# A four-layer decoder: layer 2's experts in a hand-written order with two result tables, routing steps at the units' ends, shared experts spread, the activation table load tied

## Chip, cores and metric

One core of one Trainium2 chip runs the program. The metric is the device time of one execution in microseconds (us); smaller is better. TensorE is called PE, VectorE DVE, ScalarE ACT, GpSimd POOL and SyncE SP, as in the profile.

## What is computed

The reference is a pre-norm decoder of four layers on x, 128 sequences of 64 positions and 128 features, so 8192 tokens. Every layer adds a self attention, a cross attention to `ctx_1024` and a feed-forward part to x, each of them applied to the layer norm of x. The feed-forward parts differ:

- Layer 0: 64 experts with 64 hidden features; each token goes to 8 of them, chosen within the best 4 of 8 groups of experts; and a shared expert for all tokens.
- Layer 1: a quantised gated layer with 512 hidden features.
- Layer 2: 16 experts with 512 hidden features, where each expert chooses 1024 tokens, and a shared expert with 256 hidden features.
- Layer 3: an inner block with attention, and 8 experts of which the best two count for each token.

Layer 2's experts are the centre of this case:

```python
scores = jax.nn.sigmoid(h @ gate_w.T)
cap = math.ceil(T / E * TOP_K)            # 8192 / 16 * 2 = 1024
topk_score, topk_ids = jax.lax.top_k(scores.T, cap)
xin = h[topk_ids]
up = jnp.einsum('ecd,efd->ecf', xin, up_w) + up_b[:, None, :]
g = jnp.einsum('ecd,efd->ecf', xin, gw) + gb[:, None, :]
eo = jax.nn.silu(g) * up
eo = jnp.einsum('ecf,edf->ecd', eo, down_w) + down_b[:, None, :]
flat = (eo * topk_score[..., None]).reshape(-1, Dm)
out = jnp.zeros_like(h).at[topk_ids.reshape(-1)].add(flat)
```

## The kernel before

x stays in SBUF as 64 row tiles of 128 tokens (`self.x`). Four tiles make a group (G = 4, 512 tokens), so there are 16 groups (`ng`).

**The chains.** `chain` runs the attention parts of a layer one behind the other, as a software pipeline over groups; its unit `u` is half a group. It runs under a manual schedule: every engine issues its instructions in the order in which the code emits them. For each unit it emits the weights (scores and exponentials), the maxima of the next unit, the mix with the values, the division, and, a few groups ahead, the norms (`measured` and `normed`), the transposes (`turned_in`) and the projections (`projected`). Layer norm's statistics come from DVE (lines 190 and 191), the reciprocal root from POOL (193 and 195), and the normalisation itself either from DVE (`norm`, line 215) or from ACT (`norm_act`, line 203 ff.). A chain can carry hooks: functions with a place (half, offset in units), at "a" or "b" within a unit, that do the feed-forward part's routing for a group while the attention of later groups goes on. `chain` takes a function `before`, called ahead of its loop. `feed` and `fed` load the result tables of a previous expert part and add them to x. ACT's table of functions is preloaded once per chain, by `preload_act_table_set`.

**Layer 0's experts.** `l0_ahead` makes the routing hooks. `l0_experts` runs inside the `before` of layer 1's chain, so in the same manual order. The loop takes two experts at a time: `fetch` gathers rows by an indirect DMA (line 1136), `turn` transposes them, `hidden` and `result` are the matmuls, and the results are added into two tables in DRAM by indirect DMAs with addition (line 1143), one table for either slot. The layer's shared expert is a generator whose steps are placed between these. Before the loop, layer 1's attention weights, biases and relative-position tables are prepared.

**Layer 2's experts.** After layer 2's chain, the framework's scheduler sets the order. `l2_places` finds each expert's threshold by 30 bisection steps, the ranks, and the rows that each place of an expert holds. `l2_shared` computes the shared expert and writes x to a table `rows_x` in DRAM. `l2_experts` then goes over 16 experts and two halves of four blocks of 128 tokens each. For a half it emits this:

```python
for k in range(HB):
    self.gather(xe[k], rows_n, idx[:, e, b + k : b + k + 1])
    nc.tensor.transpose(px[:, k, :], xe[k][:, 0:P], self.ident)
```

Then come the 16 hidden matmul instructions (lines 1826 and 1830), a Silu on ACT (1834), the product on DVE (1835), the result matmuls of 128 columns (1845), and four scatters with addition into the one table `rows_x`:

```python
y = sp.tile([P, P], F32, tag=f"y{k}", name=f"y{k}")
nc.vector.tensor_scalar_mul(y, py[:, k, :], xe[k][:, P + e : P + e + 1])
self.scatter_add(rows_x, y, idx[:, e, b + k : b + k + 1])
```

Gathers and scatters are issued by POOL's queue, in its order. At the end x is read back from `rows_x`, and layer 3's chain starts.

Of the kernel before, what the change touches and what calls it, by code (L numbers as in the profile page):

```python
# [8 lines left out]
F32 = mybir.dt.float32  # L9
# [52 lines left out]
class Decoder:  # L62
# [135 lines left out]
    def norm_act(self, dst, src, stats):  # L198
# [4 lines left out]
        nc.vector.scalar_tensor_tensor(  # L203
            out=nb, in0=mv[:, :, 0], scalar=-1.0, in1=rs, op0=ALU.mult, op1=ALU.mult
        )
# [31 lines left out]
    def chain(self, name, subs, hooks=None, before=None):  # L237
# [20 lines left out]
        with ExitStack() as c:  # L258
            pool = lambda *a, **k: c.enter_context(tc.tile_pool(*a, **k))
            c.enter_context(tc.manual_schedule())  # L260
            wp = pool(name=f"{name}_w", bufs=1)
            with tc.tile_pool(name=f"{name}_pw", bufs=2, space=PSUM) as self.pS:
                subs = [sub(wp) for sub in subs]
            if before is not None:
                before()
# [5 lines left out]
            nc.scalar.preload_act_table_set("natural_log_exp_and_others")  # L271
# [8 lines left out]
            for q in groups[-self.ng :]:  # L280
                q["hooks"] = {**q.get("hooks", {}), **(hooks or {})}
# [4 lines left out]
            def feed(q):  # L286
                if q["n"] < self.ng:
                    q["fed"] = []
                    for i, table in enumerate(tables):
                        add = self.gp.tile([P, G, P], F32, tag=f"fed{i}", name=f"fed{i}")  # L290
                        self.load_rows(add, table, q["g"], nc.scalar)
                        q["fed"].append(add)

            def fed(q):
                if q["n"] < self.ng:
                    xg = self.x[:, q["g"] * G : (q["g"] + 1) * G, :]
                    for add in q.pop("fed"):
                        nc.gpsimd.tensor_tensor(out=xg, in0=xg, in1=add, op=ALU.add)

            def hooked(half, u):  # L300
                for q in groups[max(0, (u - far) // 2) : u // 2]:
# [4 lines left out]
            for u in range(-10, max(nu + 6, nu + far - 1)):  # L306
# [4 lines left out]
                if odd:  # L311
                    if not linear:
                        do(self.normed, e + 3)
                else:
# [4 lines left out]
                    if not linear:  # L319
                        do(self.measured, e + 3)  # L320
# [10 lines left out]
                if odd:  # L331
                    do(self.finished, e - 1)
                    if linear:
                        do(self.normed, e + 3)
                    do(self.projected, e + 2)
                    do(self.biased, e + 2)
                else:
                    do(self.valued, e + 1)
                    do(self.turned_in, e + 2)
                    if linear:  # L340
                        do(self.measured, e + 3)
# [3 lines left out]
                if unit(u + 1):  # L345
                    self.turn_maxima(u + 1, unit(u + 1))

# [58 lines left out]
    def projected(self, q):  # L406
# [20 lines left out]
        for r in range(4):  # L427
            for h in range(4):
                rows = slice(r * 32 + h, (r + 1) * 32, 4)

                queue = nc.scalar if q["n"] == 0 and r % 2 else nc.sync
# [284 lines left out]
    def l0_attn(self, wp):  # L716
# [20 lines left out]
        for k in ("rel", "rel_r"):  # L737
            rel = wp.tile([H, 8, P], F32, tag="small", name=f"{k}_sb")
            rel = rel.rearrange("h a (b d) -> h (a b) d", d=HD)[:, 0:127, :]
            nc.sync.dma_start(out=rel, in_=self.t[k])  # L740
# [1245 lines left out]
```

## Time and profile before

| | us |
|---|---|
| median of 3 runs | 4540.99 |
| lowest and highest | 4539.59, 4547.18 |
| the profiled execution | 4533.17 |
| its span | 4531.4 |
| busy: PE, DVE, ACT, POOL | 3695.3, 2748.6, 1999.5, 1716.0 |
| busy: scatters (1143), gathers (1136) | 203.6, 201.8 |

The profile page covers one execution. Its groups give, after the bar, the busy time in us, the mean of one instruction in ns, and the idle time of the engine ahead of it with what ended it ("<-"). A timeline row is start, duration, engine, line, operation, output and inputs, count, and in brackets the idle time before. In the 40 slices a digit is the busy share in tenths; PEclk is the clock that PE was granted, in tenths of full speed. Everything that the prediction rests on comes from that one execution, whose own time stands in the table beside the median.

### The profile page before, as it was taken

The page shows a single profiled execution, that of the slowest core. Times are in us where ns is not written, and L with a number is a line of the kernel's source. Part 1 is how long each engine was busy: PE and PEld are TensorE (multiplying, and loading weights), DVE is VectorE, ACT ScalarE, POOL GpSimd, SP SyncE. Part 2 cuts the span into 40 slices and gives each one's busy share as a digit, 9 for nine tenths or more (in the row PEclk, how much of TensorE's full clock was granted, in tenths as well). Part 3 has the DMA queues.
Part 4 walks back from the last instruction along what each step waited for, and adds up shares of the span by engine and source line. Part 5 has one row for each costly group of instructions (what it writes and reads, how often), then busy time and mean ns, then how long its engine had stood idle before and what let it go on. Part 6 is the DMA issues. An engine that isn't in the chain of part 4 may idle for free. (4 is left out here: it accounts for less than half of the span.)

```text
span 4531.4 us, 157084 instructions
## 1 busy us (share of the span) xinstructions
PE 3695.3 (82%) x67053; PEld 2334.7 (52%) x67053; DVE 2748.6 (61%) x8132; ACT 1999.5 (44%) x3021; POOL 1716.0 (38%) x2762
## 2 busy tenths in 40 slices
PE   5999884776999885447999887688875899889979
PEld 3665552333555553224666654355443566556656
DVE  4665664445777996886556647333321666678766
ACT  2555552112444443334777773111111686447822
POOL 2333554675332444001222222355554223863221
PEclk9999996557999997568999999888887899999989
DMA  3112223342111221000011112122232211101111
GB/s 86 36 42 65 81 77 80 83 80 65 51 41 44 64 61 44 1 1 29 31 36 59 63 57 75 50 52 52 52 58 33 70 35 43 45 30 51 50 50 36
DMA packets 262678, 233.12 MB, mean 51 GB/s; under 512 B 66974, under 2 KB 191031, under 8 KB 261981
## 3 DMA queue, kind: packets, MB, share of 16 engines
q1 hardware_dynamic: 167996, 157.44, 11.1%
q0 software_dynamic: 35104, 29.41, 4.5%
q10 hardware_dynamic: 58880, 36.22, 2.7%
q8 instruction: 530, 8.68, 0.8%
q14 instruction: 168, 1.37, 0.1%
HBM read 93.13 MB, written 58.47 MB: 33 GB/s over the span
## 5 line engine op out<-in xcount | busy, mean ns | idle before, releaser
L610 ACT ACTIVATE p<-st 128x1024 f32<-128x1024 f32 x512 | 522.2, 1020 | 479.6 <-PE st L588 453.7
L575 PE MATMUL st<-qx,kT 64*64 64x256 f32 x9216 | 652.1, 392 | 68.3 <-ACT p L605 37.2
L515 DVE TENSOR_REDUCE m<-ps 128x8 f32<-128x512 f32 x896 | 555.0, 681 | 251.4 <-PE ps L500 250.7
L575 PEld LDWEIGHTS st<-qx,kT 64*64 64x64 f32 x9216 | 324.3, 133 | 231.5 <-issue 60.4
L522 POOL CAST mx<-m 128x32 bf16<-128x32 f32 x256 | 54.5, 213 | 1002.9 <-DVE m L515 1002.8
L628 PEld LDWEIGHTS po<-p,vx 128*32 128x32 f32 x18432 | 287.4, 110 | 224.8 <-issue 221.9
L628 PE MATMUL po<-p,vx 128*32 128x64 f32 x18432 | 380.9, 223 | 0.8 <-ACT p L610 0.8
L193 POOL TENSOR_SCALAR ve<-mv 128x4 f32<-128x4 f32 x256 | 58.9, 230 | 848.3 <-DVE mv L191 835.8
L500 PE MATMUL ps<-kx,qT 32*64 32x256 f32 x8192 | 317.9, 390 | 19.1 <-ACT vx L471 10.1
L637 PE MATMUL po<-p,consts 128*32 128x128 f32 x8192 | 319.6, 274 | 0.0
L1143 POOL DMA_INDIRECT l_rows_x<-y,l_idx x128 | 203.6, 1591 | 239.5 <-DMA l_rows_x<-y,l_idx 172.5
L195 POOL TENSOR_TENSOR rs<-ve,neghalf 128x4 f32<-128x4 f32 x256 | 266.1, 1039 | 21.3
L588 PEld LDWEIGHTS <-pick 32*64 32x64 bf16 x8192 | 134.2, 104 | 222.9 <-issue 222.7
L1136 POOL DMA_INDIRECT xe<-l_rows_n,l_idx x192 | 201.8, 1051 | 107.3 <-issue 41.5
L215 DVE TENSOR_SCALAR xn<-x,mv,rs 128x128 f32<-128x128 f32 x576 | 221.8, 441 | 29.7 <-POOL rs L195 29.7
L588 PE MATMUL st<-mT,pick 32*64 32x128 bf16 x8192 | 214.0, 221 | 23.9 <-DVE mT L538 23.6
L190 DVE BATCH_NORM_STATS2 st<-x 128x6 f32<-128x128 f32 x768 | 202.8, 266 | 47.8 <-DMA x<-l_rows_x 30.0
L500 PEld LDWEIGHTS ps<-kx,qT 32*64 32x64 f32 x8192 | 183.6, 133 | 90.4 <-issue 56.7
L660 DVE TENSOR_TENSOR e<-po,r 128x256 f32<-128x256 f32 x256 | 107.3, 419 | 191.3 <-ACT r L658 186.6
L637 PEld LDWEIGHTS po<-p,consts 128*32 128x32 f32 x8192 | 208.4, 111 | 0.1
L538 DVE COPY mT<-ps 128x256 bf16<-128x256 bf16 x256 | 73.5, 287 | 216.8 <-PE ps L534 216.5
L191 DVE BATCH_NORM_AGGREGATE mv<-st 128x2 f32<-128x6 f32 x1024 | 182.4, 180 | 30.9
(410 smaller groups left out, 7745.6 us busy)
## 6 DMA issues: line engine op xcount, KB each, us to landing
qx<-qT SPq DMA_DIRECT2D x2272, 16.0 KB
kx<-kT SPq DMA_DIRECT2D x512, 64.0 KB
cT<-in_ctxT SPq DMA_DIRECT2D x64, 256.0 KB
l_rows_n<-fn ACTq DMA_DIRECT2D x32, 256.0 KB
l_turned<-fT ACTq DMA_DIRECT2D x32, 256.0 KB
l_rows_y<-zeros SPq DMA_DIRECT2D x32, 256.0 KB
fed<-l_rows_y ACTq DMA_DIRECT2D x32, 256.0 KB
x<-in_x SPq DMA_DIRECT2D x16, 256.0 KB
```

What stands on the lines that cost most here:

```text
L190: nc.vector.bn_stats(st[:, i, :], src[:, i, :])
L195: nc.gpsimd.tensor_tensor(out=rs, in0=ve, in1=self.neghalf, op=ALU.pow)
L215: self.nc.vector.tensor_scalar(out=dst[:, i, :], in0=src[:, i, :], scalar1=mv[:, i, 0:1], scalar2=rs[:, i : i + 1], op0=ALU.subtract, op1= ...
L500: nc.tensor.matmul(ps[r][s * S : (s + 1) * S, i * 256 : (i + 1) * 256], lhsT=qT[f, k], rhs=kx[f, :, k], start=mask != "causal", stop=mask ...
L515: nc.vector.tensor_reduce(m[:, :, r, :], ps[r].rearrange("p (t h k) -> p t h k", t=2, k=S), AX.X, ALU.max)
L575: nc.tensor.matmul(st[o * S : (o + 1) * S, a, :].rearrange("p (j s q) -> p j s q", s=2, q=S)[:, :, s, :], lhsT=kT[f, k], rhs=qx[f, o:8:2, ...
L588: nc.tensor.matmul(st[o * S : (o + 1) * S, a, j * P : (j + 1) * P], lhsT=self.pick[f, 2 * j + o, :], rhs=q["mT"][f, i, :], start=False, st ...
L610: nc.scalar.activation(p, s0, AF.Exp, scale=1.0 if mask == "bias" else scale)
L628: nc.tensor.matmul(po[e * 32 : (e + 1) * 32, 0, i, s * S : (s + 1) * S], lhsT=vx[:, k, j, :], rhs=p[j // 4][:, j % 4, s * S : (s + 1) * S] ...
L637: nc.tensor.matmul(po[e * 32 : (e + 1) * 32, 1, i, :], lhsT=self.spread_sum[:, jp, :], rhs=p[e // 2][:, (2 * e + jp) % 4, :], start=jp == ...
L1136: self.nc.gpsimd.indirect_dma_start(out=dst, out_offset=None, in_=table, in_offset=bass.IndirectOffsetOnAxis(ap=idx, axis=0), bounds_check ...
L1143: self.nc.gpsimd.indirect_dma_start(out=table, out_offset=bass.IndirectOffsetOnAxis(ap=idx, axis=0), in_=src, in_offset=None, bounds_check ...
```

## The change

**Norms, chain and hooks.** The offset of `norm_act` goes from one DVE operation to two on POOL; layer 1's two attentions and the norm inside its cross attention use `norm_act`. The table preload is tied to its place. Hooks get a third place "c" at the unit's end; layer 0's routing is cut into 18 steps with new places, and the last two groups use a `late` list. `measured` and `normed` can run early, at a unit's end. The adds of the result tables go to DVE for the first two groups. `spare` is called in the units behind a chain's last. The first group's qx transfers use three queues. Layer 1's relative-position tables are loaded in hooks of layer 0.

```diff
         nb = self.sm.tile([P, G], F32, name="nb")
-        nc.vector.scalar_tensor_tensor(
-            out=nb, in0=mv[:, :, 0], scalar=-1.0, in1=rs, op0=ALU.mult, op1=ALU.mult
-        )
+        nc.gpsimd.tensor_tensor(out=nb, in0=mv[:, :, 0], in1=rs, op=ALU.mult)
+        nc.gpsimd.tensor_scalar_mul(nb, nb, -1.0)
...
+            table = lambda: nc.scalar.preload_act_table_set("natural_log_exp_and_others")
+            if before is None:
+                tc.keep_in_program_order(table())
...
+                before(setup)
+                table()
...
-            nc.scalar.preload_act_table_set("natural_log_exp_and_others")
...
+                own = late if late and i >= self.ng - 2 else hooks
+                q["hooks"] = {**q.get("hooks", {}), **(own or {})}
...
+                    engine = nc.vector if q["n"] < 2 else nc.gpsimd
                     for add in q.pop("fed"):
-                        nc.gpsimd.tensor_tensor(out=xg, in0=xg, in1=add, op=ALU.add)
+                        engine.tensor_tensor(out=xg, in0=xg, in1=add, op=ALU.add)
...
+                if now and not linear:
+                    if odd:
+                        once(self.measured, e + 4)
+                    else:
+                        once(self.normed, e + 3)
+                hooked("c", u)
+                if spare is not None and u >= nu + 4:
+                    spare(u - nu - 4)
...
-                queue = nc.scalar if q["n"] == 0 and r % 2 else nc.sync
+                queue = [nc.sync, nc.scalar, nc.gpsimd][(4 * r + h) % 3] if q["n"] == 0 else nc.sync
...
+            hooks={("c", 2): load, ("c", 4): table, ("c", 5): spread},
```

The `norm="act"` argument and its use:

```diff
+            mask="bias", scale=RSQRT8, kind="softmax", norm="act",
...
+        norm = self.norm_act if q.get("norm") == "act" else self.norm
+        norm(z, z, q["z_stats"])
...
+            norm="act",
```

The routing's places (letter, and units after the group's first):

```diff
+        parts = "c3 b4 b5 b6 c6 b7 b8 c8 b9 c9 b10 c10 b11 c11 c12 b13 c13 b14".split()
+        late = "c3 b4 c4 b5 c5 a6 b6 c6 a7 b7 c7 a8 b8 c8 a9 b9 c9 a10".split()
```

**The shared expert** is one generator for layers 0 and 2. In layer 0 groups 0 to 7 are done in the chain's tail (`spare`), 8 to 10 ahead of the places, 11 to 15 in the expert loop. `add_y` adds to x as before. Layer 1's setup is called in the middle of the loop.

```diff
+    def shared(self, groups, turned, w, nsh, tiles):
+        nc = self.nc
+        wg, wu, wd = w
+        items = [(g, k) for g in groups for k in range(nsh)]
+        xT, sg = {}, {}
+        def load(g):
+            xT[g] = tiles("xT")
+            nc.sync.dma_start(out=xT[g], in_=turned[g])
+        load(items[0][0])
+        for i in range(len(items) + 2):
+            if i < len(items):
+                g, k = items[i]
+                if k == nsh - 1 and g + 1 in groups:
+                    load(g + 1)
+                ps = self.place()
+                nc.tensor.matmul(
+                    ps, lhsT=wg[:, k * P : (k + 1) * P], rhs=xT[g], start=True, stop=True
+                )
+                sg[g, k] = tiles("sg")
+                nc.scalar.activation(sg[g, k], ps, AF.Silu)
+                yield
+            if 0 < i <= len(items):
+                g, k = items[i - 1]
+                ps = self.place()
+                nc.tensor.matmul(
+                    ps, lhsT=wu[:, k * P : (k + 1) * P], rhs=xT[g], start=True, stop=True
+                )
+                nc.vector.tensor_tensor(out=sg[g, k], in0=ps, in1=sg[g, k], op=ALU.mult)
+                yield
+            if i > 1 and items[i - 2][1] == nsh - 1:
+                g = items[i - 2][0]
+                py = self.place().rearrange("p (t d) -> p t d", d=P)
+                for t in range(G):
+                    for k in range(nsh):
+                        nc.tensor.matmul(
+                            py[:, t, :], lhsT=sg[g, k][:, t * P : (t + 1) * P], rhs=wd[:, k, :],
+                            start=k == 0, stop=k == nsh - 1,
+                        )
+                self.add_y(g, py)
...
             do = lambda f, j: f(j) if 0 <= j < n else None
-            steps = shared()
+            steps = self.shared(range(11, self.ng), turned, w, 1, tiles)
             for j in range(-5, n + 2):
                 do(fetch, j + 3)
+                do(find, j + 5)
+                do(turn, j + 1)
                 do(result, j - 1)
                 next(steps, None)
-                do(find, j + 5)
-                do(turn, j + 1)
-                if j % 2:
-                    next(steps, None)
                 do(hidden, j)
+                if j == n // 2:
+                    setup()
```

**Layer 2.** `l2` becomes `l2_l3`, and the expert part moves into the `before` of layer 3's chain, in manual order. `rows_x`, its filling and the reload of x go; two tables are zeroed in the hook `put` and added to x by layer 3's chain. `l2_shared` goes. In `l2_places` a copy is split over ACT and DVE, the quota's loads move to ACT's queue, both masks come ahead of the quota, the ranks are bf16, and the search for rows takes three blocks at a time. The bias of the result is added by ACT, from a bias transposed in the layout; the bias matmul goes.

```diff
+                    for table in tables:
+                        nc.sync.dma_start(
+                            out=table[g * W : (g + 1) * W, :].rearrange("(t p) d -> p t d", p=P),
+                            in_=bc(z, 1, G),
+                        )
...
+                hooks = dict(zip([("c", 3), ("b", 4), ("b", 5), ("b", 6)], steps, strict=True))
+                late = dict(zip([("c", 3), ("b", 4), ("c", 4), ("b", 5)], steps, strict=True))
...
-        nc.vector.tensor_copy(scT, ps)
+        nc.scalar.copy(scT[:, 0:4, :], ps[:, 0:4, :])
+        nc.vector.tensor_copy(scT[:, 4:8, :], ps[:, 4:8, :])
...
-            nc.sync.dma_start(
+            nc.scalar.dma_start(
```

The new functions of `l2_experts` and its loop:

```diff
+            def fetch(q):
+                q["xe"] = []
+                for k in range(HB):
+                    xe = sp.tile([P, P + E], F32, tag=f"xe{k}", name=f"xe{k}", bufs=3)
+                    self.gather(xe, rows_n, idx[:, q["e"], q["b"] + k : q["b"] + k + 1])
+                    q["xe"].append(xe)
+            def turn(q):
+                px = self.place().rearrange("p (k t) -> p k t", t=P)
+                for k in range(HB):
+                    nc.tensor.transpose(px[:, k, :], q["xe"][k][:, 0:P], self.ident)
+                q["xT"] = sp.tile([P, HB, P], F32, tag="xT", name="xT")
+                nc.scalar.copy(q["xT"], px)
+            def hidden(q):
+                e = q["e"]
+                wg, wu, wd = weights[e]
+                hT = q["hT"] = sp.tile([P, NC, HB, P], F32, tag="hT", name="hT", bufs=1)
+                for f in range(NC):
+                    pg = pG.tile([P, HB, P], F32, tag="pg", name="pg")
                     nc.tensor.matmul(
-                        py, lhsT=self.ones3, rhs=bc(db3[:, e, :], 1, HB), start=True, stop=False
+                        pg, lhsT=wg[:, f * P : (f + 1) * P], rhs=q["xT"], start=True, stop=True
                     )
-                    for k in range(HB):
-                        for f in range(NC):
-                            nc.tensor.matmul(
-                                py[:, k, :], lhsT=hT[:, f, k, :], rhs=wd[:, f, :],
-                                start=False, stop=k == HB - 1 and f == NC - 1,
-                            )
-                    for k in range(HB):
-                        y = sp.tile([P, P], F32, tag=f"y{k}", name=f"y{k}")
-                        nc.vector.tensor_scalar_mul(y, py[:, k, :], xe[k][:, P + e : P + e + 1])
-                        self.scatter_add(rows_x, y, idx[:, e, b + k : b + k + 1])
-ORDER = ["l0_l1", "l1_ffn", "l2", "l3"]
+                    pu = pU.tile([P, HB, P], F32, tag="pu", name="pu")
+                    nc.tensor.matmul(
+                        pu, lhsT=wu[:, f * P : (f + 1) * P], rhs=q["xT"], start=True, stop=True
+                    )
+                    sg = sp.tile([P, HB, P], F32, tag="sg", name="sg")
+                    nc.scalar.activation(sg, pg, AF.Silu, bias=gb[:, e, f : f + 1])
+                    nc.vector.scalar_tensor_tensor(
+                        out=hT[:, f, :, :], in0=pu, scalar=ub[:, e, f : f + 1], in1=sg,
+                        op0=ALU.add, op1=ALU.mult,
+                    )
+            def result(q):
+                wd = weights[q["e"]][2]
+                ps = self.place()
+                for f in range(NC):
+                    nc.tensor.matmul(
+                        ps, lhsT=wd[:, f, :], rhs=q["hT"][:, f, :, :],
+                        start=f == 0, stop=f == NC - 1,
+                    )
+                q["yT"] = sp.tile([P, HB * P], F32, tag="yT", name="yT", bufs=1)
+                nc.scalar.activation(
+                    q["yT"], ps, AF.Identity, bias=db[:, q["e"] : q["e"] + 1]
+                )
+            def back(q):
+                e = q["e"]
+                py = pY.tile([P, HB, P], F32, tag="py", name="py")
+                for k in range(HB):
+                    nc.tensor.transpose(py[:, k, :], q["yT"][:, k * P : (k + 1) * P], self.ident)
+                for k in range(HB):
+                    y = sp.tile([P, P], F32, tag=f"y{k}", name=f"y{k}", bufs=1)
+                    nc.vector.tensor_scalar_mul(y, py[:, k, :], q["xe"][k][:, P + e : P + e + 1])
+                    self.scatter_add(tables[k % 2], y, idx[:, e, q["b"] + k : q["b"] + k + 1])
+            do = lambda f, g: f(steps[g]) if 0 <= g < n else None
+            shared = self.shared(range(self.ng), turned, (wsg, wsu, wsd), 2, tiles)
+            per = 2 * nb // HB
+            search = iter(())
+            do(fetch, 0)
+            do(fetch, 1)
+            for g in range(-1, n + 2):
+                if (g + 1) % per == 0 and (g + 1) // per + 1 < E // 2:
+                    search = finding((g + 1) // per + 1, sp)
+                next(search, None)
+                do(turn, g + 1)
+                next(shared, None)
+                do(result, g - 1)
+                next(search, None)
+                do(hidden, g)
+                next(shared, None)
+                do(back, g - 1)
+                next(shared, None)
+                do(fetch, g + 2)
+                if g >= 0 and g % 2 == 1 and g // 2 + 1 < E:
+                    load(g // 2 + 1)
+                if g == n // 2:
+                    setup()
```

```diff
+ORDER = ["l0_l1", "l1_ffn", "l2_l3"]
```

## The prediction

> **What bounds the kernel now.** I read the page first (busy time in 40 slices), then the groups and the timeline of the stage with the lowest clock, then the windows of single stages.
>
> ```profile
> PE   5999884776999885447999887688875899889979
> POOL 2333554675332444001222222355554223863221
> PEclk9999996557999997568999999888887899999989
> ```
>
> PE carries the program (82%), except in two stretches: slices 6 to 9 (layer 0's routing tail and experts, clock down to 5 tenths) and 25 to 30 (layer 2's experts, 2889 to 3510 us: 621 us, 32 steps of four blocks), where POOL, which issues gathers and scatters, is busiest. By form, in 2850 to 3515:
>
> ```profile
> L1143 POOL DMA_INDIRECT l_rows_x<-y,l_idx x128 | 203.6, 1591 | 239.5 <-DMA l_rows_x<-y,l_idx 172.5 <-DVE hT L1835 24.1 <-issue 19.2
> L1845 PE MATMUL py<-wd,hT 128*128 128x128 f32 x1024 | 163.3, 327 | 0.0
> L1826 PE MATMUL pg<-xT,wg 128*128 128x512 f32 x256 | 146.6, 656 | 9.9 <-ACT xT L1822 9.1
> L1136 POOL DMA_INDIRECT xe<-l_rows_n,l_idx x128 | 133.4, 1042 | 45.9 <-issue 32.1 <-DVE l_idx L1777 4.9 <-DVE x L710 2.9
> ```
>
> The scatters wait 172.5 us for the scatter before them on the one table. The timeline of one step:
>
> ```profile
> 3066.68 1.56 POOL L1143 DMA_INDIRECT l_rows_x<-y,l_idx  x1 [2.04 <-DMA l_rows_x<-y,l_idx]
> ...
> 3070.72 1.55 POOL L1143 DMA_INDIRECT l_rows_x<-y,l_idx  x1 [2.48 <-DMA l_rows_x<-y,l_idx]
> 3072.57 1.09 POOL L1136 DMA_INDIRECT xe<-l_rows_n,l_idx  x1 [0.30 <-issue]
> 3073.97 1.06 POOL L1136 DMA_INDIRECT xe<-l_rows_n,l_idx  x1 [0.31 <-issue]
> ...
> 3075.34 0.45 PE L1820 MATMUL px<-consts,xe 128*128 128x128 f32 x1 [3.88 <-DMA xe<-l_rows_n,l_idx]
> ...
> 3075.58 5.34 PE L1845 MATMUL py<-wd,hT 128*128 128x128 f32 x26
> ...
> 3077.97 1.63 POOL L1143 DMA_INDIRECT l_rows_x<-y,l_idx  x1 [0.30 <-issue]
> ...
> 3083.75 1.02 PE L1826 MATMUL pg<-xT,wg 128*128 128x512 f32 x2
> 3084.61 1.02 PE L1830 MATMUL pu<-xT,wu 128*128 128x512 f32 x2
> 3085.46 1.02 PE L1826 MATMUL pg<-xT,wg 128*128 128x512 f32 x2
> ...
> 3108.10 2.16 PE L1845 MATMUL py<-wd,hT 128*128 128x128 f32 x17
> ```
>
> The reader sees scatters 4.0 us apart, gathers 1.4 apart, a gather landing 2.8 us after its start (3072.57 to 3075.34), a pair of 512-wide matmuls every 0.86 us, and PE at work between: POOL's and PE's parts lie beside each other, 18.6 us a step. Layer 0's loop has two tables already; its scatters:
>
> ```profile
> 881.78 1.62 POOL L1143 DMA_INDIRECT l_rows_y<-y,l_idx  x1 [0.57 <-DVE y L1485]
> 883.71 1.58 POOL L1143 DMA_INDIRECT l_rows_y<-y,l_idx  x1 [0.30 <-issue]
> ```
>
> 1.93 apart. Last, windows of layer 1's cross attention (three groups) and layer 2's (three groups); columns are PE, PEld, DVE, ACT, POOL, clock:
>
> ```profile
> 1594.80:1662.20 67.40, 57.52 (x1474) 37.76 (x1478) 61.74 (x138) 30.09 (x45) 32.87 (x55) 0.95 0.21 62
> 2549.30:2611.00 61.70, 53.91 (x1347) 37.57 (x1346) 38.08 (x115) 46.67 (x71) 18.03 (x45) 1.00 0.21 67
> ```
>
> **Layer 2's experts, the term that decides.** Two tables take away the wait of 2.0 to 2.5 us per scatter. But the loop is now in a fixed order. Iteration g issues turn(g+1), result(g-1), hidden(g), back(g-1), fetch(g+2), with the shared expert between. fetch(g+2) feeds turn(g+2), the first PE work of the next iteration. On POOL its gathers stand behind the four scatters of back(g-1), whose y need the transposes at the end of PE's work in iteration g. PE issues in order, so it stands at turn until those gathers land; POOL stands until PE is through. Before, the scheduler's order let the next gathers go ahead of the last scatter (3072.57 stands before 3077.97). The two parts now add up:
> - POOL: first scatter 0.3 after its y; four scatters 1.93 to 1.99 apart, to the first gather 7.9; to the fourth gather 1.40 + 1.36 + 1.31 = 4.1; landing 2.8. Sum 15.1 us.
> - PE at full clock: last transpose 0.15; result, now 8 matmuls of 512 columns, 8 x 0.43 = 3.4; hidden, 16 x 0.43 = 6.9; four transposes and y 1.0; places of rows 0.3; up to three parts of the shared expert, 2.4. Sum 14.2.
> - Clock: after the gap of 3.88 us above, 26 matmuls took 5.34 us, 205 ns each, against 2.16 / 17 = 127 later: 2.0 us lost. The new gap of some 15 us comes in every step. The Trainium skill, "TensorE: Matmul & The Clock Gate" (Part 1: The HAM clock gate), says that the array drops to half clock after an idle window of about 3.4 us, and gets full clock back after as long of sustained work. That speaks against this change: half of 3.4 is 1.7 us lost per step. I take 2.2, since the pauses of result and y come within the warm-up; the rule would make the sum 15 us smaller over 29 steps.
>
> So T = 31.5 us with the shared expert (its 80 parts last for 24 of the 29 steady steps), 29.2 without: 24 x 31.5 + 5 x 29.2 = 902. Filling and draining: 12 gathers before the second turn (four are repeated) 16 + 3, first two short iterations some 32, last results and scatters 15, half clock 8: 74. Stage 976 against 621: **+355**. Low end: mean T 27 if the scatters come at their bare 1.6 and the clock loses nothing: +236. High end 32.5: +395.
>
> **The other parts.**
> - Layer 0's cross attention with routing hooks runs at 25 us a group, against 18.9 before hooks begin. PE is busy 90.3 of 105 us there, 21.5 a group. Steps at unit ends wait less: I take 22.5, 12 groups x -2.5 = **-30** (0 to -42).
> - Layer 0's tail and experts: weights of layer 1 were prepared in 759 to 781, POOL and PE idle: -22. The 32 steps of 7.65 us lose most of the shared expert (5 groups of 16 stay): 1.05 each, -33. Coming back: setup inside the loop +8, shared groups and table switches ahead of it +9. **-38** (-10 to -60).
> - Layer 1, norms to ACT: DVE loses 4 x 0.441 us a group (L215), and in cross attention 4 x 0.339 more. Self attention (21.2 a group, PE 19.6) closes 1.25 of its gap: 16 x -1.25 = **-20** (0 to -28). Cross attention is DVE's: 61.74 / 3 = 20.6 falls to 17.5, PE's 19.2 then ends it, with 1.3 of gaps 20.5 for 22.5: **-30** (0 to -50). The two POOL operations for nb lie beside PE; if POOL were late they would cost about 1 us a group.
> - Layer 2's cross attention: four table loads of 1283 ns a group (below) leave ACT, which is at 46.67 / 3 = 15.6 against PE's 18.0; PE waits for ACT's p. 20.6 goes to 18.9: **-26** (0 to -41). The same loads in layer 3 and layer 2's self attention lie under PE: layer 3's self attention with them takes 16.5 a group, as layer 0's without. The skill, "ScalarE: Activation LUTs" (What ACT_TABLE_LOAD costs), adds a drain of about 1.38 us to each switch; this trace has only 2.3 us idle before 128 loads. By the page 10.6 us a group would go instead of 5.1, and layer 2 would come to PE's 18.0: -41.
>
> ```profile
> L657 ACT ACT_TABLE_LOAD x128 | 164.2, 1283 | 2.3
> ```
>
> - Layer 2's places: 31 counts in 88.5 us lose the shared expert beside them, 2.86 to 2.5: -11; threshold and quota on two queues -7 (quota ended 8.2 of wait); bf16 ranks, one find instead of two, shorter tail -11. **-29** (-10 to -40).
> - Into layer 3: no reload of x, but two adds and two loads per group, as at layer 1, where the seam took 16.5 (1048.4 to 1064.9) against 10.5 here: **+6** (0 to +10). The zeroing (two writes of 256 KB a group on SP) and the loads on ACT's queue are as in layers 0 and 1 today, where groups of self attention keep their time: nothing; without that cover 1 us a group.
> - qx on three queues for the first group, table load tied: **-6** (0 to -10).
>
> Sum: -30 - 38 - 20 - 30 - 26 - 29 + 6 - 6 = -173; with +355, +182. The profiled execution took 4533.2 (span 4531.4 and 1.8 around it), so 4715; the median of the runs is 7.8 above it: **4723**.
>
> **Rivals.**
> - *The gathers do overlap* (faster). Three buffers for xe suggest a fetch ahead of need. If gathers were on POOL before the scatters, T would be PE's 14.2 plus gaps, 15: 74 + 29 x 15 = 509, -112, total 4541 - 173 - 112 = 4256. For it: before, POOL did run ahead. Against it: fetch(g+2) and turn(g+2) have only back(g-1) and the iteration's edge between them. It decides from T = (621 + 173 - 74) / 29 = 24.8 us downwards: at most 8 of POOL's 15 us may stay exposed. Chance 0.08.
> - *Serial, but cheaper*: T 27, other parts as summed: 4541 - 173 + 236 = 4604. With the other parts at -230 as well it would be no change. For it: L1143's mean is 1.59. Against it: 0.3 to 0.4 of issue shows before every one. Chance 0.12, of which 0.02 no change.
> - *The gains fail*: attention stays where PE's own gaps hold it, and only setup, shared expert and places pay, -85: 4541 - 85 + 355 = 4811. Chance 0.10.
>
> **How the numbers follow.** The main case has 0.70. Its own terms give T 29.5 to 32.5 and gains of -130 to -210: about 4640 to 4800; taking in part of the cheap case and the failed gains, the range is 4620 to 4815. Measurement of this kernel can tell about 0.2%, 9 us, from no change. Faster 0.08, same 0.02, slower 0.90.
>
> **What would show it.** Layer 2's stage at 31 us a step; PE idle some 15 us in each, ended by a gather at the transpose; clock near 0.7 to 0.8 there; no scatter waiting for its table; POOL idle until y. Table loads down from 256 to a few; layer 1's cross attention at 20.5, layer 2's at 18.9. I am wrong if gathers stand ahead of a step's scatters, or if PE's gap per step is under 8 us.

## The result, and the profile after

The changed kernel is slower: 4820.23 us median of 4 runs (4814.99 to 4826.6), against 4540.29 for the kernel before; the ratio is 1.062, 95% interval 1.059 to 1.065. The direction and the main cause were forecast, but the time lies 5 us above the top of the range and 97 above the predicted 4723. The profiled execution has a span of 4824.5, 293.1 more than before. The table splits that at the first and last keys (ACT's kT) of each stage, in us:

| stage | before | after | change | predicted |
|---|---|---|---|---|
| start | 53.4 | 41.0 | -12.4 | -6 |
| layer 0, self attention | 261.9 | 270.9 | +9.0 | 0 |
| layer 0, cross attention | 349.6 | 354.8 | +5.2 | -30 |
| layer 0's tail and experts | 400.0 | 359.1 | -40.9 | -38 |
| layer 1, self attention | 336.5 | 335.0 | -1.5 | -20 |
| layer 1, cross attention and FFN | 676.3 | 737.1 | +60.8 | -30 |
| layer 2, self attention | 297.1 | 296.1 | -1.0 | 0 |
| layer 2, cross attention | 297.8 | 264.0 | -33.8 | -26 |
| layer 2's places and experts, to layer 3's keys | 848.5 | 1161.3 | +312.8 | +332 |
| layer 3 | 1010.3 | 1005.3 | -5.0 | 0 |

First the page of the changed kernel, 40 slices:

```profile
PE   6999887459997664479999545556555699889989
POOL 3234555853324451012233123333333443773221
PEclk9999887579998885679999667777777799999989
```

Slices 24 to 31, counted from 0, are layer 2's experts: PE at 5 to 6 tenths, POOL at 3 to 4, so neither is full. The groups of that stage (2830 to 3805) say why:

```profile
L1187 POOL DMA_INDIRECT l_rows_y<-y,l_idx x128 | 206.3, 1612 | 585.4 <-DVE y L1953 536.1 <-issue 30.8 <-DMA l_rows_y<-y,l_idx 13.3
L1937 PE MATMUL ps<-hT,wd 128*128 128x512 f32 x256 | 146.9, 727 | 0.0
L1180 POOL DMA_INDIRECT xe<-l_rows_n,l_idx x132 | 137.4, 1041 | 168.5 <-DVE thr L1790 128.5 <-issue 37.8 <-DMA xe<-l_rows_n,l_idx 0.9
L1908 PE MATMUL ps<-consts,xe 128*128 128x128 f32 x128 | 56.7, 456 | 372.1 <-DMA xe<-l_rows_n,l_idx 372.1
```

The wait for the table fell from 172.5 to 13.3 us, as it should with two tables. In its place POOL stands 536.1 us for y, the end of PE's work, and PE stands 372.1 us for the gathers. Each waits for the other in turn. One step in the timeline (start, duration):

```profile
3048.03 4.69 PE L1937 MATMUL ps<-hT,wd 128*128 128x512 f32 x8
...
3061.39 1.12 DVE L1953 TENSOR_SCALAR y<-py,xe 128x128 f32<-128x128 f32 x4 [0.48 <-PE py L1950]
3062.02 1.63 POOL L1187 DMA_INDIRECT l_rows_y<-y,l_idx  x1 [17.58 <-DVE y L1953]
...
3063.95 1.57 POOL L1187 DMA_INDIRECT l_rows_y<-y,l_idx  x1 [0.30 <-issue]
...
3066.08 1.55 POOL L1187 DMA_INDIRECT l_rows_y<-y,l_idx  x1 [0.56 <-issue]
3068.07 1.55 POOL L1187 DMA_INDIRECT l_rows_y<-y,l_idx  x1 [0.44 <-issue]
3069.93 1.08 POOL L1180 DMA_INDIRECT xe<-l_rows_n,l_idx  x1 [0.31 <-issue]
...
3072.76 0.45 PE L1908 MATMUL ps<-consts,xe 128*128 128x128 f32 x1 [10.33 <-DMA xe<-l_rows_n,l_idx]
```

The reader sees y, four scatters 2.0 apart, the first gather 7.9 after the first scatter, its rows at PE 2.8 later, and PE idle for 10.33 until then. The mean step is 31.5 us over the first 24 and 28.8 over the next five.

The second surprise is in layer 1's cross attention, 27.9 us a group (here and below the mean of the ten middle groups, between their kT). The window holds three groups (length; PE, PEld, DVE, ACT, POOL busy; clock; share of the DMA engines, GB/s):

```profile
1500.00:1582.90 82.90, 60.84 (x1513) 38.87 (x1515) 43.29 (x114) 39.63 (x69) 36.16 (x67) 0.88 0.17 51
```

DVE fell from 61.7 us in three groups (the prediction's window) to 43.3, as meant, but no engine is busy for more than three quarters. Groups of that window, then its timeline:

```profile
L604 PE MATMUL st<-qx,kT 64*64 64x256 f32 x192 | 15.9, 452 | 19.9 <-ACT p L639 19.9
...
L206 ACT ACTIVATE xn<-x,nb,rs 128x128 f32<-128x128 f32 x12 | 4.9, 482 | 13.6 <-POOL nb L204 13.6
...
L851 POOL TENSOR_TENSOR z<-z,spread 128x512 f32<-128x512 f32 x3 | 3.8, 1265 | 12.3 <-ACT z L206 12.3
```

```profile
1511.99 1.65 ACT L206 ACTIVATE z<-z,nb,rs 128x128 f32<-128x128 f32 x4
...
1513.73 1.26 POOL L851 TENSOR_TENSOR z<-z,spread 128x512 f32<-128x512 f32 x1 [4.11 <-ACT z L206]
1515.07 1.26 POOL L852 TENSOR_TENSOR z<-z,spread 128x512 f32<-128x512 f32 x1
1516.41 1.26 POOL L854 TENSOR_TENSOR x<-x,z 128x512 f32<-128x512 f32 x1
1517.63 0.20 POOL L203 TENSOR_TENSOR nb<-mv,rs 128x4 f32<-128x4 f32 x1
...
1518.17 1.65 ACT L206 ACTIVATE xn<-x,nb,rs 128x128 f32<-128x128 f32 x4 [4.53 <-POOL nb L204]
1519.72 1.00 ACT L639 ACTIVATE p<-st 128x1024 f32<-128x1024 f32 x1
```

It is one chain through two queues: ACT norms z; POOL's three operations on z wait for that; nb, 0.44 us of work, stands behind them; ACT's norm of x waits for nb; the exponential stands behind the norm; PE waits for the exponential (19.9 us in three groups).

### The profile page after: what moved, and what is told of

Same layout as the page of the kernel before. It is cut to its first block, busy times and chain, and to the rows that moved or that the text cites. A ratio compares the mean times of both kernels' runs of the same rounds, so it can differ in the third digit from the quotient of the medians.

```text
span 4824.5 us, 155558 instructions
## 1 busy us (share of the span) xinstructions
PE 3672.1 (76%) x66245; PEld 2258.1 (47%) x66253; DVE 2670.4 (55%) x8008; ACT 1772.2 (37%) x2957; POOL 1778.2 (37%) x2972
## 5 line engine op out<-in xcount | busy, mean ns | idle before, releaser
L604 PE MATMUL st<-qx,kT 64*64 64x256 f32 x9216 | 672.5, 400 | 106.9 <-ACT p L639 70.8
L1187 POOL DMA_INDIRECT l_rows_y<-y,l_idx x192 | 309.4, 1611 | 611.4 <-DVE y L1953 536.1
L604 PEld LDWEIGHTS st<-qx,kT 64*64 64x64 f32 x9216 | 334.4, 136 | 276.1 <-ACT p L639 77.0
L1908 PE MATMUL ps<-consts,xe 128*128 128x128 f32 x128 | 56.7, 456 | 372.1 <-DMA xe<-l_rows_n,l_idx 372.1
L1927 DVE SCALAR_TENSOR_TENSOR hT<-pu,ub,sg 128x512 f32<-128x512 f32 x128 | 96.1, 751 | 284.4 <-PE pu L1922 149.7
L1908 PEld LDWEIGHTS ps<-consts,xe 128*128 128x128 f32 x128 | 22.7, 181 | 406.2 <-issue 279.1
```

The lines of the kernel that those rows point to most:

```text
L604: nc.tensor.matmul(st[o * S : (o + 1) * S, a, :].rearrange("p (j s q) -> p j s q", s=2, q=S)[:, :, s, :], lhsT=kT[f, k], rhs=qx[f, o:8:2, ...
L1187: self.nc.gpsimd.indirect_dma_start(out=table, out_offset=bass.IndirectOffsetOnAxis(ap=idx, axis=0), in_=src, in_offset=None, bounds_check ...
```

## The experiments

Each comparison of totals without an interval rests on one execution, and the executions of a kernel that was timed several times lie 9 to 28 us apart; so small effects are read from the stages of the trace and not from the total. "The changed kernel" is the one with the whole change.

**Offset nb on DVE again** (`nb_dve`).

```diff
-        nc.gpsimd.tensor_tensor(out=nb, in0=mv[:, :, 0], in1=rs, op=ALU.mult)
-        nc.gpsimd.tensor_scalar_mul(nb, nb, -1.0)
+        nc.vector.scalar_tensor_tensor(
+            out=nb, in0=mv[:, :, 0], scalar=-1.0, in1=rs, op0=ALU.mult, op1=ALU.mult
+        )
```

> The changed kernel with the offset nb of norm_act made on DVE in one operation again. Theory 1 (nb waits on POOL's queue behind the three 1.26 us operations on z, and ACT's exponential waits behind the norm that needs nb): layer 1's cross attention falls from 27.5 us a group to 20 to 22, layer 0's cross attention with hooks from 27 to 23 to 25; total about 4700, -90 to -130 against the changed kernel's 4820. Rival (the norms on ACT themselves make the exponential late): layer 1's cross attention stays above 26, total within 15 us of 4820.

Measured: 4715.98 us, 1.037 of the kernel before (1.033 to 1.040), 104 less than the changed kernel. Layer 1's cross attention takes 22.3 us a group, layer 0's with hooks 20 to 24. Of the 106 us between the two profiled executions, layer 0's cross attention holds 43.8 and layer 1's, with the FFN, 54.3. So nb on POOL costs what the prediction missed. In layer 1's ten middle groups PE is idle for 2.7 us a group in place of 7.4; the other 0.9 us is PE's own work at a clock of 0.95 in place of 0.87. Cross attention has the ACT norms still, and ACT is no longer late by nb, so the rival falls.

**nb on POOL alone, in the kernel before** (`nb_pool`).

```diff
-        nc.vector.scalar_tensor_tensor(
-            out=nb, in0=mv[:, :, 0], scalar=-1.0, in1=rs, op0=ALU.mult, op1=ALU.mult
-        )
+        nc.gpsimd.tensor_tensor(out=nb, in0=mv[:, :, 0], in1=rs, op=ALU.mult)
+        nc.gpsimd.tensor_scalar_mul(nb, nb, -1.0)
```

> The kernel before with one part of the change alone: nb of norm_act as two operations on POOL. Theory 1 (POOL's queue is long only where routing or z's operations stand in it): layer 0's cross attention with hooks rises from 25 to 26 to 28 us a group, all others stay; total +10 to +40 on 4540. Rival (nb on POOL is harmless here and hurts only with the new places of the routing steps): within 8 us of 4540.

Measured: 4670.32, +132, much more than expected. Layer 0's cross attention goes from 25.1 to 32.9 us a group, and layer 2's, which has no z and which I had expected to stay, from 20.6 to 23.9. Two different things lie behind this. In layer 0 (560 to 596) it is POOL's order: the routing norm's nb stands behind ten operations of the routing, from the first line here to the second:

```profile
573.61 1.17 POOL L1209 TENSOR_TENSOR cmp<-cmp 128x128 f32<-128x128 f32 x3
...
579.06 0.20 POOL L203 TENSOR_TENSOR nb<-mv,rs 128x4 f32<-128x4 f32 x1
...
579.61 1.65 ACT L206 ACTIVATE fn<-x,nb,rs 128x128 f32<-128x128 f32 x4 [4.28 <-POOL nb L204]
```

In layer 2 (2640 to 2665) it is not:

```profile
2656.70 0.23 POOL L193 TENSOR_SCALAR ve<-mv 128x4 f32<-128x4 f32 x1 [2.64 <-DVE mv L191]
2657.01 1.04 POOL L195 TENSOR_TENSOR rs<-ve,neghalf 128x4 f32<-128x4 f32 x1
2658.12 0.20 POOL L203 TENSOR_TENSOR nb<-mv,rs 128x4 f32<-128x4 f32 x1
2658.41 0.24 POOL L204 TENSOR_SCALAR nb<-nb 128x4 f32<-128x4 f32 x1
2658.69 1.65 ACT L206 ACTIVATE fn<-x,nb,rs 128x128 f32<-128x128 f32 x4 [2.48 <-POOL nb L204]
2660.78 1.02 ACT L609 ACTIVATE p<-st 128x1024 f32<-128x1024 f32 x1 [0.44 <-ACT fn L206]
```

What stands ahead of nb here is the root of the same norm, which nb needs on any engine. The kernel before has the same wait, a little shorter:

```profile
2562.29 0.16 DVE L203 SCALAR_TENSOR_TENSOR nb<-mv,rs 128x4 f32<-128x4 f32 x1 [0.28 <-POOL rs L195]
2562.49 1.65 ACT L207 ACTIVATE fn<-x,nb,rs 128x128 f32<-128x128 f32 x4 [2.07 <-DVE nb L203]
```

ACT waits 2.48 us for nb in place of 2.07, and PE behind it 2.47 for p in place of 2.12. The rest of the 3.4 us a group is the clock. Three groups, and 6.8 us behind the wait shown above:

```profile
2572.46:2644.26 71.80, 62.87 (x1345) 42.65 (x1345) 37.57 (x111) 47.31 (x70) 19.35 (x51) 0.86 0.18 58
2661.50:2668.30 6.80, 6.44 (x43) 4.08 (x44) 1.87 (x4) 4.73 (x7) 1.89 (x4) 0.50 0.17 55
```

PE needs 62.9 us for what took it 53.9 at full clock in the kernel before (2549.3 to 2611, in the prediction). In the ten middle groups PE's idle time grows by 0.4 us a group and its busy time by 2.9; each of these groups has one such stretch at half clock, and in the kernel before none has. nb is all that differs, so 0.4 us more on ACT's path has brought the half clock with it. In the changed kernel layer 2's cross attention takes 17.8 us a group with nb on POOL, with PE never idle, and layer 0's 25.8. What hides nb there, the hooks' new places or the tied table, was not separated.

**Gathers ahead of the scatters** (`fetch_ahead`).

```diff
-                    xe = sp.tile([P, P + E], F32, tag=f"xe{k}", name=f"xe{k}", bufs=3)
+                    xe = sp.tile([P, P + E], F32, tag=f"xe{k}", name=f"xe{k}", bufs=4)
...
             do(fetch, 0)
-            do(fetch, 1)
...
                 do(turn, g + 1)
+                do(fetch, g + 2)
...
                 do(back, g - 1)
                 next(shared, None)
-                do(fetch, g + 2)
```

> The changed kernel with the gathers of step g+2 of layer 2's experts issued right after turn(g+1), ahead of the scatters of step g-1, with four buffers for xe instead of three, and without the repeated fetch(1). Theory 1 (POOL's and PE's parts of a step add up only because the gathers stand behind the scatters): a step falls from 31.5 to 15 to 18 us, the stage from 971 to 510 to 600 us, total 4380 to 4460. Rival (the step is long since PE runs at half clock and carries the shared expert, or since scatters and gathers collide): a step stays above 24 us, total above 4600.

Measured: 4384.9, 435 less than the changed kernel. The steady step is 15.9 us (mean of 29). The same matmuls and scatters are done, and the same gathers but for the four repeated ones; their order differs, and xe has a fourth buffer. The window of the stage, and one step:

```profile
2900.00:3340.00 440.00, 415.00 (x1321) 203.00 (x1320) 195.40 (x567) 128.26 (x195) 287.79 (x217) 0.98 0.36 67
```

```profile
3064.49 1.01 POOL L1180 DMA_INDIRECT xe<-l_rows_n,l_idx  x1 [0.30 <-PE pg L1918]
...
3068.75 1.63 POOL L1187 DMA_INDIRECT l_rows_y<-y,l_idx  x1 [3.25 <-DVE y L1953]
3068.78 0.60 PE L1908 MATMUL ps<-consts,xe 128*128 128x128 f32 x4
```

PE is busy 415 of 440 us at a clock of 0.98, and its transposes start while the scatters before them have just begun. This is the prediction's "gathers do overlap" rival, which it had put at 15 us a step.

**More work for PE inside its wait** (`warm`).

```diff
+                if 0 <= g < n:
+                    warm = self.place()
+                    for _ in range(15):
+                        nc.tensor.matmul(
+                            warm, lhsT=wsg[:, 0:P], rhs=weights[steps[g]["e"]][0], start=True, stop=True
+                        )
                 do(turn, g + 1)
```

> The changed kernel with 15 more matmuls (128x128 by 128x512, result not read) ahead of turn(g+1) in each of layer 2's expert steps, where PE otherwise waits for the gathers; it changes no result. Theory 1 (the wait ends on POOL, and PE's work behind it runs its first part at half clock): the added 13 us lie in the wait, the work behind it runs at full clock, and a step gets 1.5 to 3 us shorter, total 4735 to 4785. Rival (PE's own work is the bound, or the clock costs nothing): a step gets no shorter, or up to 13 us longer, total 4820 to 5200.

Measured: 4826.03, no gain in total. Windows of the changed kernel and of this one:

```profile
2880.00:3570.00 690.00, 400.81 (x1108) 191.82 (x1108) 169.76 (x504) 104.03 (x158) 231.94 (x175) 0.76 0.19 37
```

```profile
2910.00:3600.00 690.00, 651.48 (x1834) 302.74 (x1833) 176.70 (x525) 108.59 (x165) 238.95 (x180) 0.98 0.20 38
```

PE does 250 us more in the same time: it was waiting. The clock goes from 0.76 to 0.98, and the result matmuls (L1937, x248 in each) from a mean of 732 to 616 ns. The step falls from 31.0 to 29.8 (means of 29), by 1.2 us, less than the 1.5 to 3 expected. That is not yet the price of the half clock, as the added matmuls outlast the wait:

```profile
3053.67 13.14 PE L1969 MATMUL ps<-wg,wsg 128*128 128x512 f32 x30
...
3063.77 1.01 POOL L1180 DMA_INDIRECT xe<-l_rows_n,l_idx  x1 [0.30 <-issue]
...
3066.65 0.60 PE L1908 MATMUL ps<-consts,xe 128*128 128x128 f32 x4
```

From the start of the fourth gather to the last transpose it is now 3.1 us on average, for 2.7 in the changed kernel, and POOL's part is 0.1 longer. What PE does behind the last transpose, up to y, falls from 15.3 to 13.5: so the half clock costs 1.8 us a step, where I took 2.2. The total gains nothing, as the added matmuls also stand where nothing hides them (first scatter 26 us later, the last full step 23.6 for 10.7).

**Table load tied, alone, in the kernel before** (`table`).

```diff
+            tc.keep_in_program_order(
+                nc.scalar.preload_act_table_set("natural_log_exp_and_others")
+            ) if before is None else None
             c.enter_context(tc.manual_schedule())
...
-            nc.scalar.preload_act_table_set("natural_log_exp_and_others")
+            if before is not None:
+                nc.scalar.preload_act_table_set("natural_log_exp_and_others")
```

> The kernel before with one part of the change alone: the preload of ACT's table tied ahead of the manual order, for the chains without a function ahead of their loop (layers 0, 2 and 3). Theory 1 (in layer 2's cross attention ACT is late by its table loads): the 256 loads fall to a few, that stage falls from 20.5 to 17.7 us a group, total -30 to -45 against 4540. Rival (the loads lie in ACT's idle time, and the stage's gain in the changed kernel came from the earlier norms): the stage stays above 20 us, total within 10 us of 4540.

Measured: 4519.47, 0.9935 of the kernel before (0.991 to 0.996), 25 less. The loads fall from 265 to 9, but layer 2's cross attention only to 19.4 us a group: a part of the gain, between theory and rival.

**Both mendings** (`fetch_nb`: the edits of `fetch_ahead` and `nb_dve`).

> The changed kernel with both mendings: the gathers of step g+2 ahead of the scatters of step g-1 (four buffers for xe, no repeated fetch), and nb of norm_act on DVE in one operation. Theory 1 (two causes, in different stages): the gains add, 440 and 102 us, total 4270 to 4295, 0.940 to 0.947 of the kernel before. Rival (they share something, such as DVE's load or the clock): the gains overlap, total above 4320.

Measured: 4273.35, 0.940 (0.938 to 0.942). 435 and 104 add up to 539 of the 547 gained: two separate causes.

**One table, with the gathers ahead** (`one_table`: `fetch_nb`, and the edit below).

```diff
-                    self.scatter_add(tables[k % 2], y, idx[:, e, q["b"] + k : q["b"] + k + 1])
+                    self.scatter_add(tables[0], y, idx[:, e, q["b"] + k : q["b"] + k + 1])
```

> As fetch_nb, but all scatters of layer 2's experts go to the first of the two tables (the second stays zero; the sum is the same). Theory 1 (with the gathers ahead, PE bounds the step at 15.7 us, and POOL's part must stay below): four scatters 4 us apart and four gathers make 21 us, POOL bounds again, a step takes 19 to 22 us, the stage 100 to 200 us more than in fetch_nb, total 4380 to 4480. Rival (the order alone made the gain, and the wait for the table lies beside PE): a step stays below 17 us, total within 30 us of fetch_nb.

Measured: 4405.4, +132; the step is 20.0 for 16.0 us. POOL's group (2750 to 3270):

```profile
L1188 POOL DMA_INDIRECT l_rows_y<-y,l_idx x102 | 161.7, 1586 | 236.0 <-DMA l_rows_y<-y,l_idx 117.5 <-DVE hT L1928 39.0 <-DVE y L1954 26.6
```

The wait for the table is back (117.5) and is the longest of POOL's. So the second table is worth 4 us a step with the gathers ahead. What it is worth in the changed kernel's own order was not run.

**Layer 1's norms** (`z_dve`: `fetch_nb` with z normed by `norm`, so on DVE; `l1_dve`: both of layer 1's attentions without `norm="act"` as well).

```diff
-        norm = self.norm_act if q.get("norm") == "act" else self.norm
-        norm(z, z, q["z_stats"])
+        self.norm(z, z, q["z_stats"])
```

> As fetch_nb, but in layer 1's cross attention the norm of z is on DVE and only the norm of x on ACT. Theory 1 (with both on ACT, PE's wait there is for ACT's exponential, as it was for DVE's maxima with both on DVE): the stage falls from 21.8 to 20 to 21 us a group, total 10 to 30 us below fetch_nb. Rival (PE waits for the round trip of z through DRAM and POOL, wherever the norms are): 21.5 to 22.5 us a group, total within 8 us of fetch_nb.

> As fetch_nb, but all norms of layer 1's two attentions on DVE, as in the kernel before. Theory 1 (moving the norms to ACT is worth nothing: self attention's wait is a chain from the scores over DVE's maxima to POOL, which has no norm in it, and in cross attention one wait takes the place of another): self attention 21.2 and cross attention 21.5 to 22.5 us a group, total within 15 us of fetch_nb. Rival (the prediction's step: DVE is late by its load): self attention stays at 21.2 but cross attention rises to 23 or more, total over 20 us above fetch_nb.

Measured: 4262.34 and 4277.15. Layer 1's self attention is 21.2 us a group in all of them. Cross attention takes 22.2 with both norms on ACT, 22.6 with both on DVE, 20.4 with one on each. Four groups with both on ACT (kernel `nb_dve`), and four with one on each (`z_dve`):

```profile
1450.00:1538.80 88.80, 77.73 (x1980) 50.83 (x1984) 59.02 (x161) 52.38 (x92) 45.08 (x72) 0.96 0.21 62
```

```profile
1450.00:1531.60 81.60, 73.38 (x1978) 48.77 (x1977) 67.02 (x173) 46.22 (x77) 45.68 (x73) 1.00 0.23 68
```

Neither engine was overloaded (52.4 and 59.0 of 88.8 us). Of the 7.2 us between the two windows, 4.4 are PE's busy time for the same work, at a clock of 0.96 in place of 1.00, and 2.8 its idle time. With both on ACT, PE waits for the exponential behind them; in `nb_dve` (1450 to 1539):

```profile
L605 PE MATMUL st<-qx,kT 64*64 64x256 f32 x264 | 18.2, 389 | 8.0 <-ACT p L640 8.0
```

**What else gave layer 2 its gain** (`l2_hooks`: `z_dve` with layer 2's hooks at b4, a5, b5, a6; `no_early`: `z_dve` without the early calls of `measured` and `normed`).

> As z_dve, but layer 2's four routing hooks at their old places (b4, a5, b5, a6). Theory 1 (of the 2.9 us a group that layer 2's cross attention gained, the tied table gave 1.2, and the later places of the hooks the rest): that stage rises from 17.8 to 19 to 19.6 us a group, total +15 to +30 on z_dve. Rival (the rest came from the norms at the units' ends): it stays at 17.6 to 18.1, total within 8 us of z_dve.

> As z_dve, but without the early calls of measured and normed at the units' ends (they run at their old places). Theory 1 (hooks' places matter, not these): all self attention stages stay within 0.2 us a group, layer 2's cross attention at 17.6 to 18.1, total within 15 us of z_dve. Rival (the early norms made the rest of layer 2's gain): layer 2's cross attention rises to 19 or more, and others by 0.5 and more, total +20 to +60.

Measured: 4280.54 and 4254.38. With the old places layer 2's cross attention takes 19.4 us a group, without the early norms 17.8, as in `z_dve`. Four groups of `z_dve`, and of `l2_hooks`:

```profile
2400.00:2471.00 71.00, 71.00 (x1792) 49.79 (x1788) 50.09 (x153) 43.04 (x76) 24.55 (x60) 1.00 0.35 107
```

```profile
2400.00:2477.50 77.50, 71.07 (x1792) 49.35 (x1792) 51.03 (x153) 43.45 (x76) 25.23 (x60) 1.00 0.32 98
```

With the new places PE has no idle time left at all. The early norms are worth nothing that these runs can tell.

**The best version** (`best`: `z_dve`, with `spread` collected in a list and issued in the first two spare units).

```diff
-                    nc.gpsimd.dma_start(
-                        out=self.rel[k].rearrange("h (t u) -> h t u", u=127), in_=bc(q["tab"], 1, S)
-                    )
+                    self.spreads.append(lambda k=k, q=q: nc.gpsimd.dma_start(
+                        out=self.rel[k].rearrange("h (t u) -> h t u", u=127), in_=bc(q["tab"], 1, S)
+                    ))
...
+                    if self.spreads:
+                        self.spreads.pop(0)()
                     for k in range(6 if i < 5 else 99):
```

> As z_dve, and the two writes of layer 1's relative-position tables (spread, POOL's queue) moved from layer 0's self attention into the two first spare units behind layer 0's chain. Theory 1 (the write of many short pieces slows the qx transfers of the group, for which PE then waits): the two long groups of layer 0's self attention (19 to 23 and 21.3 us) fall to 16.5, total 5 to 12 us below z_dve's 4262, 0.934 to 0.939 of the kernel before. Rival (the reduction on DVE or the load makes them long): they stay, total within 4 us of z_dve.

Measured: 4254.38, 0.937 of the kernel before (0.936 to 0.938), the fastest of those that were timed more than once. In the changed kernel a long group of layer 0's self attention looks so:

```profile
138.52 15.88 SPq L461 DMA_DIRECT2D qx<-qT  x16
...
140.77 0.86 POOL L784 DMA_DIRECT2D rel_scratch<-rel_tab  x1
...
150.14 1.97 PE L529 MATMUL ps<-kx,qT 32*64 32x256 f32 x20 [3.05 <-issue]
```

In `best` no group there is longer than 16.7 us, and the stage, from the first keys to layer 0's first cross keys, takes 260.9. It takes 267.3 in `z_dve`, 266 to 272 in the ten kernels here that have the write in this place, and 261.9 in the kernel before. So it is the write that makes the groups long; the totals of `best` and `z_dve` cannot be told apart. How it reaches PE is open. PE's row above stops in the middle of matmuls that read kx and qT, not qx, and the profile names no wait for it ("issue").

## Why the prediction was right or wrong

- **Layer 2's experts: right.** "The two parts now add up": a step of 31.5 with the shared expert and 29.2 without was forecast, 31.5 and 28.8 came, and places and experts together moved by +313 for +332. Inside the sum small errors cancel, so the exact hit on 31.5 is in part luck. Over the first 24 steps POOL's part, from y to the last transpose, took 15.8 us for 15.1, and PE's part behind it 15.7 for 16.4. The half clock is 1.8 of that (`warm`) and not 2.2. The rule of the Trainium skill that was weighed there ("TensorE: Matmul & The Clock Gate", Part 1: The HAM clock gate) had led to an estimate of 1.7, which agrees. PE's waits for gathers add up to 372 us in 32 steps, about 12 each and not 15, as the last part of the shared expert runs beside the first scatters and the transposes come between the gathers.
- **"The two POOL operations for nb lie beside PE; if POOL were late they would cost about 1 us a group": the step that failed.** They cost 5.6 us a group in layer 1's cross attention (27.9 against 22.3), and 7.8 and 3.4 in layers 0 and 2 in the kernel before. I had priced two short operations by their time and asked only about layer 1. In layers 0 and 1 their price is the wait for whatever stands ahead of them on POOL (the routing, z's operations), plus what stands behind the norm on ACT. In layer 2 their own 0.4 us came through to PE and brought the half clock with it; the prediction had a clock term for the experts and none for the attention. In the changed kernel nb costs 104 us in all, as much as the whole miss of 97. With nb on DVE the total is 4716, near the predicted 4723, and that is luck: layer 1's cross attention still misses its gain by 37 us and its self attention by 21, layer 0's self attention is 8 longer, and other stages make up for it.
- **Layer 1's gains (-20 and -30): wrong as well.** Self attention gained 1.5. Its gap before the transposed maxima comes from a chain (scores, four adds and maxima on DVE, POOL's split) that contains no norm, so a lighter DVE does not shorten it. In cross attention a wait for DVE became one for ACT, even with nb mended: over the ten middle groups PE waits 31 us for DVE in the kernel before, and 20 for ACT's p and 7 for its xT in `fetch_nb`. What is to be had there, 19 us (307.4 for 326.5 between the first and last keys), needs one norm on each engine (`z_dve`).
- **Layer 0's hooks (-30): hidden, not wrong.** +5.2 came; with nb on DVE the stage takes 310.9 for 349.6, so -39. What I left out is `spread`: a DMA of a moved step, on a queue that I did not follow. Self attention took 9 us longer, and in `best`, with the write moved, 1 us less than before the change.
- **Layer 2's cross attention: right in size, half in cause.** -33.8 for -26. The tied table gives 1.2 us a group, the hooks' new places 1.6. ACT was late by table loads, and by where the norm stood.
- **Start, layer 0's tail, places, seam**: off by 23 us together, nearly all to the good. The gathers of layer 2 start 173 us after its last cross keys, for 217 before, -44 for the forecast -29; the seam cost +7 for +6.
- **The range** held only mishaps in the gains that ended at zero. A term that the trace of before did not show, nb on POOL, was put at about 1 us a group and not at the longest wait in the queue it was moved to.
- **The page** was read too simply: slices 15 to 17 (layer 1's FFN) are a third stretch with PE at 4 to 5 tenths, and POOL is busiest in slice 34. No term of the sum hangs on either.

## What to carry to other kernels

In a fixed order, ask of every moved instruction what stands ahead of it on the new queue and what stands behind its reader, and ask whether a slightly longer wait of PE will lower its clock: 0.44 us of work moved to POOL cost 132 us in the kernel before. In a loop with loads, work and stores on in-order queues, put the next loads ahead of the stores, with one more buffer: it made 31 us into 16. Judge a moved norm by PE's idle time and by its clock, not by the busy time of the engine it left.

## What the runs showed of the hardware that was not expected

- Keeping PE at work through its wait raised the granted clock from 0.76 to 0.98. PE's work behind the wait took 13.5 us in place of 15.3, and the step 29.8 in place of 31.0.
- A wait of PE of 2.5 us in each group of layer 2 (`nb_pool`) went with 6.8 us at half clock a group and a mean of 0.86; with 2.1 us in the kernel before, the same stage has a mean of 1.00. These waits are shorter than the idle window of about 3.4 us that the prediction cites from the Trainium skill ("TensorE: Matmul & The Clock Gate", Part 1: The HAM clock gate), so that window is no safe bound here.
- Beside the write of the relative-position table (rel_scratch, issued by POOL) the sixteen qx transfers (issued by SP, on another queue) took 15.88 us to issue, against 10.87 for the sixteen in the next group.
